# A graph network's edge loop on one core: tiles of 128 edges instead of 125, and the row-by-row and early gathers left out

## The chip, the core and the metric

The kernel runs on one core of a Trainium2 chip. The core has five engines that run side by side, each in the order of its own instructions: PE (matrix products, with weight loads shown apart as PEld), DVE (elementwise work), ACT (functions and copies), POOL (here: gathers) and SP (here: it issues DMA transfers). Sixteen DMA engines move data between HBM and the core's memory, SBUF. The metric is the device time of one execution in microseconds; less is better.

## The reference

One layer of a graph network with attention, on 12,500 nodes of 64 features and 412,500 edges, sorted by receiver:

```python
h = jnp.maximum(_layernorm(x, axis=-1), 0.0)
msg_in = jnp.concatenate([h[src], h[dst], edge_attr_32], axis=-1)
messages = swish(msg_in @ W1 + b1) @ W2 + b2
att = softmax(swish(msg_in @ Wa1 + ba1) @ Wa2 + ba2, axis=0)   # over all edges
aggregated = segment_sum(messages * att, dst, 12500)
out = x + swish(concatenate([h, aggregated]) @ Wu1 + bu1) @ Wu2 + bu2
```

All numbers are 32-bit floats.

## The kernel before, in words

**Node stage.** The node features are normalised in chunks, and two tables of 128 numbers a node are written to HBM: `ts_d`, a node's share of the first layer as a sender, and `tr_d`, its share as a receiver. The transposed features stay in SBUF as `hT`.

**Tiles and groups.** The edges are cut into tiles of `EP` = 125, one edge to a partition, and `K` = 8 tiles make a group: 3304 tiles, 413 groups (`NG`), the last one padded. The main loop in `one_pass` goes over the groups. In iteration g it runs `begin(g)`, then `load(g + 2)` (`AHEAD` = 2), then `end(g)`, and between them the steps of `sum_up` for a group some five back. An order written out by hand (`pin`) holds PE, DVE and ACT to the order of the text.

**load(g).** POOL gathers the sender rows: one indirect DMA per tile (L608), each fetching a row of `ts_d` for every edge into the group's buffer `gs`, of which the pool `gather` has seven. SP issues, every fourth group, the transposed edge features (`eo`, L619) and the receivers' numbers (`dbs`, L622), and for every group two loads of a window of `tr_d` (`wins`, L629; three buffers). DVE turns receivers into a one-hot matrix (L636), and PE multiplies it with the window (L640) into PSUM `pe`, which gives receiver and edge shares for all eight tiles.

**begin(g), end(g).** DVE adds `pe` and `gs` (L657), ACT takes the tanh (L662). `end(g)` makes messages and attention logits on DVE (L672 to L683); after it the group's `gs` is free, and POOL may fill it for a later group.

**sum_up.** DVE makes a weight matrix (L726), PE sums the messages by receiver (L732) and projects them (L743), and DVE adds them to a running table (L757, L761).

**Tiles that POOL doesn't gather.** There are three kinds.

- In the groups of `chosen` (g % 5 is 1 or 4, from 8 to 400: 157 groups) the last tile is made by ACT: it copies one column of `hT` per edge into `cols` (L514), 125 copies in five lots, which `burst` spreads over the iterations before. `numbers` loads the senders (`num`), `places` works out the column numbers on DVE (L497 to L503), DVE keeps the half that counts (L648), and PE multiplies by `stack` (L649).
- In every eighth group (51 of them) another tile is loaded row by row: `rows` has SP issue one DMA per edge (L558), 16 a group, with the row's number read into a register first (L552). `begin` adds that tile by itself (L659).
- The first `RAW` = 4 groups gather rows of `x` itself (L171), before the node stage has written `ts_d`, and `features` repeats the normalisation for those edges on DVE, ACT and PE (L579 to L593, L644).

So POOL gathers 3304 - 157 - 51 - 32 = 3064 tiles from `ts_d` and 32 from `x`. After the loop the update is made for all nodes and written out; a second function, `general`, runs only if the receivers don't fit the windows, which they do here.

Of the kernel before, what the change touches and what calls it, by code (L numbers as in the profile page):

```python
# [44 lines left out]
F32 = mybir.dt.float32  # L45
I32 = mybir.dt.int32
AF = mybir.ActivationFunctionType
# [7 lines left out]
EP = 125  # L55
# [18 lines left out]
LOTS = ((0, 24), (24, 24), (48, 24), (72, 24), (96, EP - 96))  # L74
ROUNDS = 5
SLOTS = {1: ((5, 1), (4, 0), (4, 1), (3, 0), (3, 1)), 4: ((5, 0), (5, 1), (4, 0), (4, 1), (3, 0))}
ROUND = 12582912.0
QUEUES = [(ENG.SP, 8, 0, 16)]
RAW = 4
# [12 lines left out]
def gnn_kernel(ctx: ExitStack, tc: tile.TileContext, n_edges, x, src, src_row, dst, dst_row, first, edge,  # L92
# [73 lines left out]
    raw_src = const.tile([P, RAW * K], I32, name="raw_src")  # L166
    nc.scalar.dma_start(raw_src, src[:, :RAW * K])
    raws = [gather.tile([P, K, C], F32, name="gs") for _ in range(RAW)]
    for g in range(RAW):
        for j in range(K):  # L170
            nc.gpsimd.indirect_dma_start(  # L171
                out=raws[g].rearrange("p k c -> p (k c)")[:EP, j * D:(j + 1) * D], out_offset=None, in_=x[:, :],
                in_offset=bass.IndirectOffsetOnAxis(ap=raw_src[:EP, g * K + j:g * K + j + 1], axis=0))

    with tc.tile_pool(name="node1", bufs=1) as node1, \
# [41 lines left out]
        eps = const.tile([P, 1], F32, name="eps")  # L217
# [186 lines left out]
def one_pass(tc, n_edges, v):  # L404
# [17 lines left out]
    with ExitStack() as ctx:  # L422
# [43 lines left out]
        with tc.tile_pool(name="work2", bufs=2) as work2, \  # L466
# [3 lines left out]
            pes, gss, lgs, ps_, psums, sps, pps, ees, mts, nums, cols, alone = ({} for _ in range(12))  # L470
# [11 lines left out]
            chosen = {g for g in range(8, NG - 12) if g % ROUNDS in SLOTS}  # L482

            def numbers(g):
                if g in chosen:
                    e = (g * K + K - 1) * EP
                    n = nums[g] = small.tile([P, EP], I32, name="num", bufs=3)
                    nc.sync.dma_start(n, bass.AP(tensor=v["src_row"].tensor,
                                                 offset=v["src_row"][:, e:].offset, ap=[[0, P], [1, EP]]))

            def places(g):
                if g not in chosen:
                    return
                n = nums[g]
                near = small.tile([1, EP], F32, name="near", bufs=1)
                to = small.tile([1, EP], I32, name="to", bufs=3)
                pin(nc.vector.tensor_scalar(to, n[0:1], 1, None, op0=ALU.logical_shift_right))  # L497
                m = NB // 2
                pin(nc.vector.tensor_scalar(near, to, 1.0 / m, 0.5 / m - 0.5, op0=ALU.mult, op1=ALU.add))
                pin(nc.vector.tensor_scalar(near, near, ROUND, None, op0=ALU.add))  # L500
                pin(nc.vector.tensor_scalar(near, near, ROUND, float(1 - m * P), op0=ALU.subtract, op1=ALU.mult))
                pin(nc.vector.scalar_tensor_tensor(to, to, float(P), near, op0=ALU.mult, op1=ALU.add))
                pin(nc.vector.tensor_scalar(n, n, 1, None, op0=ALU.bitwise_and))  # L503
                cols[g] = small.tile([P, EP], F32, name="cols", bufs=3), to
# [11 lines left out]
            def burst(g, k):  # L516
                for i in (3, 4, 5):
                    slots = SLOTS.get((g + i) % ROUNDS, ())
                    if (i, k) in slots:
                        columns(g + i, *LOTS[slots.index((i, k))])  # L520

            rows_at = {}
            dma = {ENG.SP: nc.sync, ENG.Activation: nc.scalar}

            def single(q, g):

                if g < NG - 4:
                    t = g * K + K - 1 - (g in chosen)
                    rows_at[q, g] = small.tile([1, EP], I32, name=f"one_src{q}", bufs=2)
                    nc.sync.dma_start(rows_at[q, g], v["src_row"][:, t * EP:(t + 1) * EP])  # L530

            def rows(q, g):
                engine, every, phase, n_rows = QUEUES[q]
                if g == 0:
                    single(q, phase + every)
                if g < phase:
                    return
                at = (g - phase) % every
                g = g - at + every
                if at == 0:  # L540
                    rows_at.pop((q, g - every), None)
                    if (q, g) in rows_at:
                        alone[g] = work2.tile([EP, C], F32, name=f"one_gs{q}")
                if at == every // 2:
                    single(q, g + every)
                if (q, g) not in rows_at:
                    return
                a = at * n_rows
                n = min(n_rows, EP - a)
                if n <= 0:  # L550
                    return
                loads, regs = nc.values_load_multi_w_load_instructions(  # L552
                    rows_at[q, g][0:1, a:a + n], engines=[engine], min_val=0, max_val=NP - 1,
                    skip_runtime_bounds_check_because=WHY)
                for one in loads:
                    pin(one)
                for k in range(n):
                    pin(dma[engine].dma_start(alone[g][a + k:a + k + 1, :], ts_d[bass.ds(regs[k], 1), :]))  # L558
# [15 lines left out]
            def features(g):  # L574

                gs = gss[g] = v["raws"][g][:EP]
                xg, xm = (gs[:, h * H:(h + 1) * H, :].rearrange("p k (r d) -> p (k r) d", d=D) for h in range(2))
                total = small.tile([EP, K], F32, name="raw_t", bufs=1)
                pin(nc.vector.tensor_reduce(total, xg, AX.X, ALU.add))  # L579
                pin(nc.vector.scalar_tensor_tensor(xm, total[:, :, None].to_broadcast([EP, K, D]), -1.0 / D, xg,  # L580
                                                   op0=ALU.mult, op1=ALU.add))
                pin(nc.scalar.activation(xg, xm, AF.Square))
                rstd = small.tile([EP, K], F32, name="raw_r", bufs=1)
                pin(nc.vector.tensor_reduce(rstd, xg, AX.X, ALU.add))
                pin(nc.scalar.activation(rstd, rstd, AF.Sqrt, bias=v["eps"][:EP], scale=1.0 / D))
                pin(nc.vector.reciprocal(rstd, rstd))
                pin(nc.vector.scalar_tensor_tensor(xg, xm, 0.0, rstd[:, :, None].to_broadcast([EP, K, D]),
                                                   op0=ALU.max, op1=ALU.mult))
                pt = one_ps.tile([P, 4, P], F32, name="mt")[:, :, :EP]
                for q in range(H):  # L590
                    pin(nc.tensor.transpose(pt[:, q, :], xg[:, 2 * q:2 * q + 2, :], ident[:EP, :EP]))
                to = raw_to[g] = v["raws"][g][:, H:, :EP]
                pin(nc.scalar.copy(to, pt))  # L593

            raw_to = {}

            def load(g):
# [4 lines left out]
                if g < RAW:  # L602
                    features(g)
                else:
                    gss[g] = gather.tile([P, K, C], F32, name="gs")[:EP]
                gs = gss[g]
                for j in range(0 if g < RAW else K - (g in chosen) - (g in alone)):
                    nc.gpsimd.indirect_dma_start(  # L608
                        out=gs[:, j, :], out_offset=None, in_=ts_d[:, :],
                        in_offset=bass.IndirectOffsetOnAxis(ap=src_sb[:, t + j:t + j + 1], axis=0))  # L610
# [20 lines left out]
                for q in range(len(QUEUES)):  # L631
                    if QUEUES[q][0] == ENG.SP:
                        rows(q, g)
# [5 lines left out]
                for q in range(H):  # L639
                    pin(nc.tensor.matmul(pe[:, 2 * q:2 * q + 2, :], eo[:, q * EP:(q + 1) * EP],  # L640
                                         win[:, q // 2, :, :], start=True,
                                         stop=g >= RAW and (q < H - 1 or g not in chosen)))
                    if g < RAW:
                        pin(nc.tensor.matmul(pe[:, 2 * q:2 * q + 2, :], raw_to[g][:, q, :], v["w_pair"][:, 0],  # L644
                                             start=False, stop=True))
# [5 lines left out]
            def begin(g):  # L651

                n = K - (g in chosen) - (g in alone)
                if g < RAW:
                    pin(nc.vector.tensor_copy(gss[g], pes[g]))
                else:
                    pin(nc.vector.tensor_tensor(gss[g][:, :n, :], pes[g][:, :n, :], gss[g][:, :n, :], ALU.add))  # L657
                if g in alone:
                    pin(nc.vector.tensor_tensor(gss[g][:, n, :], pes[g][:, n, :], alone.pop(g), ALU.add))  # L659
                if g in chosen:  # L660
                    pin(nc.vector.tensor_copy(gss[g][:, K - 1, :], pes[g][:, K - 1, :]))
# [565 lines left out]
```

## Time and profile before

| | us |
|---|---|
| median of 3 runs | 5791.38 (5784.13 to 5810.84) |
| the profiled execution | 5784.13 |
| its span, first to last instruction | 5782.4 |
| POOL's first and last gather from `ts_d` start at | 57.8 and 5679.9 |
| 16 row loads of L558, in the stretch read closely | 11.46 |
| 8 row loads of L558, a little later | 3.18 |

One line of the page is one group of instructions: its line in the code, engine, operation, what it writes and reads, the count; then the time it was busy and the mean of one in ns; then the time its engine sat idle just before, and what ended most of that. "Issue" is idle time in which the engine waited for nothing that the profile shows. The DVE's and PE's largest groups, and the DMA issues next to the row loads, are these:

```profile
L640 PE MATMUL pe<-wins,eo 128*125 128x256 f32 x3304 | 1527.2, 640 | 2546.7 <-DMA wins<-tr_d 1886.0
L726 DVE TENSOR_SCALAR wt<-iota_w,dloc,p 125x40 f32<-125x40 f32 x3304 | 759.4, 348 | 1.2
L662 ACT ACTIVATE pe<-gs 125x1024 f32<-125x1024 f32 x413 | 424.1, 1027 | 625.5 <-DMA gs<-ts_d,src_sb 189.0
...
eo<-in_edge_dram SPq DMA_DIRECT2D x103, 500.0 KB
dbs<-in_dst_row_dram SPq DMA_DIRECT2D x206, 250.0 KB
```

### The profile page before, as it was taken

To read this page: it belongs to the slowest core of one execution; us is meant where nothing else is said; L and a number is where in the kernel's file an instruction comes from. 1 tells how busy PE (TensorE), PEld (TensorE's weight loads), DVE (VectorE), ACT (ScalarE), POOL (GpSimd) and SP (SyncE) were. 2 spreads that over 40 slices of the span, in tenths; PEclk is the share of its full clock that TensorE was granted. 3 is DMA by queue.
4 is the path that set the end of the run, shared out by engine and by line. 5 is a ranking of instruction groups with operands and counts; after the bars stand their busy time and mean duration, and the time that the engine had idled before them with its cause. 6 is when DMAs were issued, how large, how long until landed. Compare 5 with 4: busy or idle time off the path is not lost. (4 is left out here: it accounts for less than half of the span.)

```text
span 5782.4 us, 108561 instructions
## 1 busy us (share of the span) xinstructions
PE 2468.3 (43%) x11609; PEld 2002.9 (35%) x11609; DVE 3466.3 (60%) x10072; ACT 2776.3 (48%) x20891; POOL 3778.6 (65%) x3121
## 2 busy tenths in 40 slices
PE   5344444444344443443444443433444443434345
PEld 4333333333333333333333333333333333333335
DVE  6565656656566655565656555655665566556657
ACT  3444444444445455454545544545455455445522
POOL 6665666666666666666667666766666666666673
PEclk8555655566555555656555556656655655655656
DMA  6233232332322223232223222222223232222233
GB/s 207 59 72 68 66 68 68 68 71 65 71 59 67 61 63 67 59 64 66 61 61 68 60 65 64 63 62 65 60 64 67 58 65 66 59 65 63 61 68 94
DMA packets 386990, 396.88 MB, mean 69 GB/s; under 512 B 235374, under 2 KB 316910, under 8 KB 385846
## 3 DMA queue, kind: packets, MB, share of 16 engines
q0 software_dynamic: 246656, 200.72, 15.9%
q1 hardware_dynamic: 138054, 179.47, 13.7%
q10 hardware_dynamic: 1520, 9.68, 0.4%
q14 instruction: 665, 5.45, 0.3%
q8 instruction: 95, 1.56, 0.1%
HBM read 360.43 MB, written 25.72 MB: 67 GB/s over the span
## 5 line engine op out<-in xcount | busy, mean ns | idle before, releaser
L608 POOL DMA_INDIRECT gs<-ts_d,src_sb x3064 | 3717.1, 1213 | 1906.6 <-issue 1794.0
L514 ACT COPY cols<-hT 128x1 f32 x19625 | 2184.3, 187 | 2078.5 <-issue 1994.7
L640 PE MATMUL pe<-wins,eo 128*125 128x256 f32 x3304 | 1527.2, 640 | 2546.7 <-DMA wins<-tr_d 1886.0
L640 PEld LDWEIGHTS pe<-wins,eo 128*125 128x125 f32 x3304 | 1017.5, 324 | 2842.9 <-issue 1835.6
L726 DVE TENSOR_SCALAR wt<-iota_w,dloc,p 125x40 f32<-125x40 f32 x3304 | 759.4, 348 | 1.2
L662 ACT ACTIVATE pe<-gs 125x1024 f32<-125x1024 f32 x413 | 424.1, 1027 | 625.5 <-DMA gs<-ts_d,src_sb 189.0
L732 PE MATMUL sp<-wt,acts 125*65 125x40 f32 x6608 | 657.7, 272 | 28.8 <-DVE wt L726 28.4
L732 PEld LDWEIGHTS sp<-wt,acts 125*65 125x65 f32 x6608 | 622.4, 188 | 35.6 <-DVE wt L726 30.0
L672 DVE SCALAR_TENSOR_TENSOR acts<-pe,gs 125x512 f32<-125x512 f32 x413 | 284.6, 689 | 408.5 <-issue 264.1
L497 DVE TENSOR_SCALAR to<-num 1x125 int32<-1x125 int32 x157 | 40.7, 259 | 778.7 <-DMA num<-in_src_row_dram 748.1
L657 DVE TENSOR_TENSOR gs<-pe,gs 125x1024 f32<-125x1024 f32 (+2 forms) x409 | 471.1, 1152 | 34.6 <-issue 10.8
L743 PEld LDWEIGHTS mt<-ss,w2u 65*128 65x128 f32 x826 | 211.8, 290 | 471.6 <-issue 375.8
L743 PE MATMUL mt<-ss,w2u 65*128 65x40 f32 x826 | 197.4, 334 | 370.0 <-DVE gm L709 145.6
L636 DVE TENSOR_SCALAR eo<-dbs,bj 64x250 f32<-64x250 int32 x826 | 294.8, 387 | 78.9 <-DMA dbs<-in_dst_row_dram 66.8
L680 DVE TENSOR_TENSOR pe<-pe,w_all 125x512 f32<-125x512 f32 x413 | 288.9, 699 | 13.8
L678 DVE SCALAR_TENSOR_TENSOR pe<-pe,gs 125x512 f32<-125x512 f32 x413 | 287.4, 696 | 10.7
L683 DVE TENSOR_REDUCE lg<-pe 125x8 f32<-125x512 f32 x413 | 284.2, 688 | 10.7
L761 DVE TENSOR_TENSOR sums<-sums,mt 64x40 f32 x606 | 115.2, 190 | 163.9 <-PE mt L743 78.6
L648 DVE SCALAR_TENSOR_TENSOR cols<-num,half,cols 128x125 f32<-128x125 int32 x157 | 54.9, 349 | 236.3 <-ACT cols L514 128.3
L764 DVE COPY stand<-nmax 64x40 f32 x826 | 186.9, 226 | 4.1 <-issue 0.8
L702 PE MATMUL mt<-ident,mx 125*128 125x125 f32 x110 | 44.6, 406 | 292.7 <-DVE sums L761 166.4
L738 ACT COPY ss<-sp 65x40 f32<-65x40 f32 x413 | 75.5, 183 | 152.3 <-remote 120.8
(140 smaller groups left out, 1230.6 us busy)
## 6 DMA issues: line engine op xcount, KB each, us to landing
one_gs<-ts_d SPq DMA_DIRECT2D x6375, 0.5 KB
eo<-in_edge_dram SPq DMA_DIRECT2D x103, 500.0 KB
dbs<-in_dst_row_dram SPq DMA_DIRECT2D x206, 250.0 KB
gs<-ts_d,src_sb POOLq DMA_INDIRECT x3064
wins<-tr_d SPq DMA_DIRECT2D x826, 32.0 KB
num<-in_src_row_dram SPq DMA_DIRECT2D x157, 62.5 KB
ts_d<-ts SPq DMA_DIRECT2D x5, 896.0 KB
tr_d<-tr ACTq DMA_DIRECT2D x5, 896.0 KB
```

What stands on the lines that cost most here:

```text
L514: pin(nc.scalar.copy(to[:, first + i:first + i + 1], hT[:, bass.ds(regs[i], 1)]))
L608: nc.gpsimd.indirect_dma_start(out=gs[:, j, :], out_offset=None, in_=ts_d[:, :], in_offset=bass.IndirectOffsetOnAxis(ap=src_sb[:, t + j:t ...
L636: pin(nc.vector.tensor_scalar(eo[:WR, e], db[:, e], bj[g // NQ % 2 * WR:(g // NQ % 2 + 1) * WR, g, h:h + 1], None, op0=ALU.is_equal))
L640: pin(nc.tensor.matmul(pe[:, 2 * q:2 * q + 2, :], eo[:, q * EP:(q + 1) * EP], win[:, q // 2, :, :], start=True, stop=g >= RAW and (q < H - ...
L657: pin(nc.vector.tensor_tensor(gss[g][:, :n, :], pes[g][:, :n, :], gss[g][:, :n, :], ALU.add))
L662: pin(nc.scalar.activation(pes[g], gss[g], AF.Tanh))
L672: pin(nc.vector.scalar_tensor_tensor(acts[g % ACTS][:, :, 0:U], th[:, :, U:C], 1.0, gs[:, :, U:C], op0=ALU.add, op1=ALU.mult))
L678: pin(nc.vector.scalar_tensor_tensor(att, th[:, :, 0:U], 1.0, gs[:, :, 0:U], op0=ALU.add, op1=ALU.mult))
L680: pin(nc.vector.tensor_tensor(att, att, wa2[:EP, None, :].to_broadcast([EP, K, U]), ALU.mult))
L726: pin(nc.vector.tensor_scalar(wt[:, j, :], iota_w[:EP, j // H, :], dloc[:, g * K + j:g * K + j + 1], p[:, k + j:k + j + 1], op0=ALU.is_equ ...
L732: pin(nc.tensor.matmul(sp, acts[g % ACTS][:, j, :], wt[:, j, :], start=j == 0, stop=j == K - 1))
L743: pin(nc.tensor.matmul(pp, w2u.rearrange("s h u -> s (h u)"), sps.pop(g), start=True, stop=True))
```

## The change

Four things change.

- `EP` becomes 128. There are 403 groups and 3224 tiles; every gather has 128 rows.
- The groups whose last tile ACT makes are one in three (`EVERY` = 3, `PHASE` = 1, groups 10 to 388: 127 of them). Six lots of 12 to 24 columns are spread over three iterations, two an iteration. `num`, `to` and `cols` have two buffers instead of three.
- The row-by-row tiles are taken out (`single`, `rows`, `QUEUES`, `alone`).
- The early gathers from `x` are taken out (`RAW`, `raws`, `features`, the extra products in `load`).

POOL gathers 3224 - 127 = 3097 tiles, all from `ts_d`. The words for the change also name the update's bias from node features in SBUF and `x` rows asked for ahead; those parts stand in both kernels alike.

```diff
-EP = 125
+EP = 128
...
-LOTS = ((0, 24), (24, 24), (48, 24), (72, 24), (96, EP - 96))
-ROUNDS = 5
-SLOTS = {1: ((5, 1), (4, 0), (4, 1), (3, 0), (3, 1)), 4: ((5, 0), (5, 1), (4, 0), (4, 1), (3, 0))}
+EVERY = 3
+PHASE = 1
+SLOTS = (((0, 24), (24, 24)), ((48, 24), (72, 12)), ((84, 24), (108, 20)))
...
-QUEUES = [(ENG.SP, 8, 0, 16)]
-RAW = 4
...
-    raw_src = const.tile([P, RAW * K], I32, name="raw_src")
-    nc.scalar.dma_start(raw_src, src[:, :RAW * K])
-    raws = [gather.tile([P, K, C], F32, name="gs") for _ in range(RAW)]
-    for g in range(RAW):
-        for j in range(K):
-            nc.gpsimd.indirect_dma_start(
...
-            chosen = {g for g in range(8, NG - 12) if g % ROUNDS in SLOTS}
+            chosen = {g for g in range(8, NG - 12) if g % EVERY == PHASE}
...
             def burst(g, k):
-                for i in (3, 4, 5):
-                    slots = SLOTS.get((g + i) % ROUNDS, ())
-                    if (i, k) in slots:
-                        columns(g + i, *LOTS[slots.index((i, k))])
-
-            rows_at = {}
...
-                for k in range(n):
-                    pin(dma[engine].dma_start(alone[g][a + k:a + k + 1, :], ts_d[bass.ds(regs[k], 1), :]))
+                for i in range(EVERY):
+                    columns(g + 3 + i, *SLOTS[EVERY - 1 - i][k])
...
-            def features(g):
...
-                if g < RAW:
-                    features(g)
-                else:
-                    gss[g] = gather.tile([P, K, C], F32, name="gs")[:EP]
-                gs = gss[g]
-                for j in range(0 if g < RAW else K - (g in chosen) - (g in alone)):
+                gs = gss[g] = gather.tile([P, K, C], F32, name="gs")[:EP]
+                for j in range(K - (g in chosen)):
...
-                for q in range(len(QUEUES)):
-                    if QUEUES[q][0] == ENG.SP:
-                        rows(q, g)
...
-                    if g < RAW:
-                        pin(nc.tensor.matmul(pe[:, 2 * q:2 * q + 2, :], raw_to[g][:, q, :], v["w_pair"][:, 0],
-                                             start=False, stop=True))
...
-                n = K - (g in chosen) - (g in alone)
-                if g < RAW:
-                    pin(nc.vector.tensor_copy(gss[g], pes[g]))
-                else:
-                    pin(nc.vector.tensor_tensor(gss[g][:, :n, :], pes[g][:, :n, :], gss[g][:, :n, :], ALU.add))
-                if g in alone:
-                    pin(nc.vector.tensor_tensor(gss[g][:, n, :], pes[g][:, n, :], alone.pop(g), ALU.add))
...
+                n = K - (g in chosen)
+                pin(nc.vector.tensor_tensor(gss[g][:, :n, :], pes[g][:, :n, :], gss[g][:, :n, :], ALU.add))
```

## The prediction

> **What bounds the kernel now.** I read the page's span and group rows first, then the waits of all engines, then SP's own waits, then the timeline of a stretch in mid-loop, and last the durations of the gather's line.
>
> ```profile
> span 5782.4 us, 108561 instructions
> PE 2468.3 (43%) x11609; PEld 2002.9 (35%) x11609; DVE 3466.3 (60%) x10072; ACT 2776.3 (48%) x20891; POOL 3778.6 (65%) x3121
> L608 POOL DMA_INDIRECT gs<-ts_d,src_sb x3064 | 3717.1, 1213 | 1906.6 <-issue 1794.0
> L514 ACT COPY cols<-hT 128x1 f32 x19625 | 2184.3, 187 | 2078.5 <-issue 1994.7
> ...
> one_gs<-ts_d SPq DMA_DIRECT2D x6375, 0.5 KB
> ```
> POOL does little but gather (L608). Each gather is 1.213 us and is followed by at least 0.305 us in which POOL waits for nothing the profile names, so one costs 1.518 us and 3064 cost 4651 us. They run from 57.8 to 5681.1 us, which is 5623 us: POOL has 972 us to spare, all of it ahead of the first gather of a group, where it waits for one of seven `gs` buffers. So POOL is close to the bound and isn't it. ACT's column copies (L514) take 2184 us busy and 1995 us of "issue" between them (their register loads): 4179 us, or 0.213 us a column. With its other work ACT has 2776 + 2085 = 4861 us.
>
> ```profile
> PE pe L640 <- DMA wins<-tr_d: 1886.0, 274, 16.2
> POOL gs L608 <- issue: 1794.0, 2933, 16.6
> ...
> SPq L558 <- DMA one_gs<-ts_d: 63.8, 152, 0.8
> SPq L558 <- DMA dbs<-in_dst_row_dram: 37.6, 46, 1.7
> ```
> The longest wait on another party is PE's: 1886 us for `wins`, a load that SP issues. SP's own waits, by contrast, come to some 290 us in the whole span (the two longest in its loop are shown). An engine whose products are waited for and that hardly waits itself sets the pace.
>
> ```profile
> 3002.65 1.46 SPq L629 DMA_DIRECT2D wins<-tr_d  x2
> 3005.20 11.46 SPq L558 DMA_DIRECT2D one_gs<-ts_d  x16
> 3010.02 1.21 POOL L608 DMA_INDIRECT gs<-ts_d,src_sb  x1 [1.56 <-issue]
> 3018.13 0.77 SPq L629 DMA_DIRECT2D wins<-tr_d  x2
> 3019.89 3.18 SPq L558 DMA_DIRECT2D one_gs<-ts_d  x8
> 3020.06 3.75 PE L640 MATMUL pe<-wins,eo 128*125 128x256 f32 x8 [7.21 <-DMA wins<-tr_d]
> ```
> This shows why. Sixteen single-row loads (L558) stand in SP's order between two groups' window loads. They took 11.46 us here (0.72 us each) and elsewhere 0.40 us each (eight in 3.18), out of a group's mean 5623/409 = 13.75 us. PE gets its window 7.21 us late, `begin`, `end` and the freeing of `gs` follow, and POOL pays at its next group.
>
> **The change, part by part.**
>
> *SP's rows go.* 6375 row loads, their 51 index loads and 408 register loads leave SP's order; at 0.40 to 0.72 us a row that is 2550 to 4590 us. What stays is two window loads a group, the edge and receiver loads every fourth group, and the numbers: under 4 us a group by the stretch above. The window is no longer late, and the 972 us of POOL's waits lose their main cause. What comes late next is whichever of POOL and ACT has more to do. The 51 tiles go back to POOL.
>
> *Columns in one group of three.* 127 groups instead of 157, 128 columns instead of 125: 16,256 copies instead of 19,625. ACT saves 3369 x 0.213 = 717 us and keeps 4144 us, 10.3 us a group. This hides behind POOL as long as POOL needs more than that. 30 tiles go back to POOL. `num` and `cols` have two buffers instead of three; a chosen group's are last read in `load`, two groups ahead of it, and the next but one asks for them only then, so I cost this at nothing; if the cover failed, SP would hold the next window back, as now.
>
> *Tiles of 128.* 403 groups instead of 413, 3224 tiles instead of 3304. PE, DVE and ACT do about the same per group (three more rows of partitions, matmuls of 128 columns instead of 125), so each saves 10/413 of its group work: 84 us of DVE's 3466. None of it is on the path.
>
> *The early gathers from x go.* 32 gathers that POOL made from 3.8 to 56.3 us, while `ts_d` was still being written (its last write is issued at 50.7 us), become 32 gathers after it. DVE, ACT and PE lose the four groups' `features`, off the path. The first gather from `ts_d` no longer stands behind them: I take 54 us for it (50.7 us and about 3 to land) instead of 57.8.
>
> *The sum of gathers.* 3224 - 127 = 3097 of 128 rows, against 3064 of 125 and the 32. POOL's work after `ts_d` is thus 3097 gathers at a price which decides everything.
>
> *The price of a 128-row gather.* No row shows one. These are the nearest:
>
> ```profile
> L608 POOL DMA_INDIRECT gs<-ts_d,src_sb x3064: 1205/1212/1549, 57.8 to 5679.9; - x192
> L171 POOL DMA_INDIRECT gs<-in_x_dram,raw_src x32: 1208/1212/3515, 3.8 to 56.3; - x32
> q0 software_dynamic: 246656, 200.72, 15.9%
> ```
> L171 gathers rows of 256 bytes and L608 of 512, at the same median of 1212 ns: bytes cost POOL nothing. Rows grow by 2.4% only. The packets say what does change. Of that queue's 246,656, each `ts_d` gather left 15 of 4096 bytes (eight rows) and 5 of 512 bytes (one row): five equal shares of 25 rows on five DMA engines. The other eleven got filler, 25 descriptors of 4 bytes each. 125 can be shared equally over 5 or 25; 128 over 2, 4, 8 or 16. If POOL's time goes by the engines that get rows, the price is at most 1212 x 16/5 = 3878 ns. If it writes all 16 engines in step, a descriptor each, the steps fall from 26 (with the closing one) to 9 and it is 1212 x 9/26 = 420 ns. Going by rows alone it is 1212 x 128/125 = 1241 ns. Bytes and rows being excluded as a large effect, the engines served are what changes by a factor, and I take it that more of them cost more. For the size I take the longest gather that L608 itself shows, 1549 ns, some 31 ns for each of eleven more engines; nothing from the far end, 242 ns an engine, supports more.
>
> The Trainium skill ("DMA: Bandwidth & Descriptors", section "Why a DMA increments its semaphore by 16 and not by 1") says that a transfer is spread over the largest number of engines, up to 16, that divides its outer size: 5 for 125 and 16 for 128. The packets agree for 125; no run here shows 128. The same page (section "Anatomy of one DMA") calls descriptor generation a small cost, with many descriptors before it shows; by that a gather stays at 1212 ns, the sum would be about 4.9 ms, and the rule speaks against my forecast.
>
> *The end.* 54 us + 3097 x (1.549 + 0.305) = 5742 us + the tail, from the last gather to the end, as now: 5782.4 - 5681.1 = 101 us. POOL then needs 14.2 us a group against ACT's 10.3, so few waits remain. I keep those now put down to ACT's columns and DVE's L680 (51.7 + 20.7 us), cut to 127/157: 60 us. That makes 5957 us of span against 5782.4. The profiled execution took 5784.13 us around its span; the median of the runs, 5791.38, lies 9 us above the span, so I forecast 5965 us.
>
> **The rivals.**
>
> *1. The gather's price goes by rows (the other side).* At 1241 ns a gather costs 1.546 us, all of them 4788 us, with head and tail 4943. POOL's 11.9 us a group stand close to ACT's 10.3, so I add 150 us of waits: about 5100 us. The constancy of 1212 ns over half the bytes speaks for it; the 16 engines speak against. It decides below a price of (5782.4 - 54 - 101 - 60)/3097 - 0.305 = 1.493 us; above that the kernel is slower.
>
> *2. The price falls.* With 420 ns POOL needs 2245 us and ACT is the bound. Its columns run from 148 us to 225 us ahead of the end now; 3462 us of them and some 560 of ACT's other 682 us (4861 - 4179), the rest lying at both ends, give 4400 us without a wait, and with waits of one us a group about 4800. The filler descriptors speak for it, the lack of any cheaper gather in the trace against.
>
> *3. SP's rows were hidden anyway.* If ACT or the chain through DVE kept the 13.75 us a group, 403 groups take 5541 us, with head and tail 5700. SP's short waits speak against.
>
> **How the numbers follow.** The forecast has 0.70: more work on POOL per gather. Rival 1 has 0.16, rival 2 0.08, rival 3 0.03, and 0.03 is left for a price within some 10 ns of 1.493 us. Two runs of this kernel differ by up to 0.5%, so no change means within 29 us. Faster is the three rivals, 0.27; same 0.03; slower 0.70. The forecast's own range is 5800 us (just past the deciding price) to 6450 (45 ns an engine, half as much again: 1.707 us a gather, 54 + 3097 x 2.012 + 101 + 60 = 6446). The whole range reaches down to 5050, which takes in rival 1 and leaves out rival 2 and the far tail above, some 2 in 10.
>
> **What would show it.** Right: the gather's row near 1.5 us or more, POOL's idle time near 3097 x 0.305 = 945 us, PE's wait for `wins` a small part of 1886 us, SP idle, 16,256 column copies. Wrong: a gather of 1.25 us or less, with POOL's waits for buffers small (rival 1) or ACT without idle time (rival 2); or windows still late with SP free (rival 3). A gap after each gather other than 0.305 us would move the sum by 31 us for every 10 ns.

## The result and the profile after

The changed kernel took 6004.51 us (median; 6000.57 to 6005.61), the kernel before beside it 5787.76 us (5773.24 to 5810.84). The ratio is 1.037, 95% interval [1.033, 1.040]: slower, by some 217 us. That is the record of the first runs, on one chip. On two chips met later the same two kernels have a ratio of 0.833; the experiments tell how far that can be explained.

The page of the changed kernel, its span, engine row, the rows of the gathers and of ACT's column copies, and the gathers' DMA queue:

```profile
span 6003.9 us, 80416 instructions
...
PE 2571.5 (43%) x11238; PEld 1997.6 (33%) x11238; DVE 3276.5 (55%) x9553; ACT 2408.1 (40%) x17477; POOL 2957.4 (49%) x3122
...
q0 software_dynamic: 99104, 203.16, 13.6%
...
L530 POOL DMA_INDIRECT gs<-ts_d,src_sb x3097 | 2940.2, 949 | 2956.7 <-issue 2880.1
L503 ACT COPY cols<-hT 128x1 f32 x16256 | 1851.3, 188 | 3085.7 <-issue 3046.2
```

A 128-row gather takes POOL 949 ns, not more than the 1213 of 125 rows but less. Its 3097 gathers, each with the 0.305 us behind it, are work for 3884 us; POOL is idle for 2957 us all the same, 2012 us more than those gaps. No engine is busy for more than 55% of the span. The packets confirm how a gather is spread: 99,104 over 3097 gathers are 32 each, 16 of 4096 bytes (eight rows) and 16 of 4 bytes, so each of the 16 engines gets eight rows. A gather of 125 rows left 80.

The waits of all engines in the same kernel (total, times, longest, in us):

```profile
ACT cols L503 <- issue: 3046.2, 3441, 2.9
POOL gs L530 <- issue: 2880.1, 3006, 31.6
...
PE mt L654 <- ACT ss L649: 1384.0, 156, 19.9
...
PE pe L559 <- DMA wins<-tr_d: 57.8, 1, 57.8
```

The 1886 us in which PE waited for windows are gone; what is left of them is one wait at the start. In their place PE waits for ACT, ACT for "issue", and POOL up to 31.6 us for a buffer. A column copy now costs (1851.3 + 3085.7)/16,256 = 0.304 us, against 0.217 before (2184.3 + 2078.5 over 19,625), with the copy itself unchanged at 188 ns. The timeline of a stretch shows where ACT's time lies:

```profile
3010.48 0.19 ACT L503 COPY cols<-hT 128x1 f32 x1 [1.22 <-issue]
3010.80 0.95 POOL L530 DMA_INDIRECT gs<-ts_d,src_sb  x1 [0.30 <-issue]
3011.88 0.19 ACT L503 COPY cols<-hT 128x1 f32 x1 [1.21 <-issue]
3012.06 0.95 POOL L530 DMA_INDIRECT gs<-ts_d,src_sb  x1 [0.30 <-issue]
...
3023.83 0.65 PE L654 MATMUL mt<-ss,w2u 65*128 65x40 f32 x2 [11.54 <-ACT ss L649]
...
3024.36 2.13 ACT L503 COPY cols<-hT 128x1 f32 x22 [0.58 <-issue]
...
3025.86 0.94 POOL L530 DMA_INDIRECT gs<-ts_d,src_sb  x1 [9.11 <-issue]
```

While POOL gathers, one every 1.25 us, ACT gets one copy done in 1.4 us. When POOL has run out of buffers, 22 copies take 2.13 us (the full pace is back at 3019.6 us, 2.9 us after the run's last gather ended). The instructions are the same. ACT is held between them, and what it owes to PE (`ss`, L649) and DVE comes late, so POOL's buffers come free late.

### The profile page after: what moved, and what is told of

Same layout as the page of the kernel before. It is cut to its first block, busy times and chain, and to the rows that moved or that the text cites. A ratio compares the mean times of both kernels' runs of the same rounds, so it can differ in the third digit from the quotient of the medians.

```text
span 6003.9 us, 80416 instructions
## 1 busy us (share of the span) xinstructions
PE 2571.5 (43%) x11238; PEld 1997.6 (33%) x11238; DVE 3276.5 (55%) x9553; ACT 2408.1 (40%) x17477; POOL 2957.4 (49%) x3122
## 3 DMA queue, kind: packets, MB, share of 16 engines
q0 software_dynamic: 99104, 203.16, 13.6%
## 5 line engine op out<-in xcount | busy, mean ns | idle before, releaser
L530 POOL DMA_INDIRECT gs<-ts_d,src_sb x3097 | 2940.2, 949 | 2956.7 <-issue 2880.1
L503 ACT COPY cols<-hT 128x1 f32 x16256 | 1851.3, 188 | 3085.7 <-issue 3046.2
L559 PE MATMUL pe<-wins,eo 128*128 128x256 f32 x3224 | 1493.4, 639 | 860.1 <-DVE eo L555 413.2
L559 PEld LDWEIGHTS pe<-wins,eo 128*128 128x128 f32 x3224 | 985.5, 323 | 1172.8 <-DVE eo L555 450.3
L637 DVE TENSOR_SCALAR wt<-iota_w,dloc,p 128x40 f32<-128x40 f32 x3224 | 723.6, 311 | 21.9 <-issue 20.1
L643 PE MATMUL sp<-wt,acts 128*65 128x40 f32 x6448 | 722.9, 293 | 15.5 <-issue 12.5
L643 PEld LDWEIGHTS sp<-wt,acts 128*65 128x65 f32 x6448 | 689.9, 213 | 16.8 <-issue 13.2
L570 DVE TENSOR_TENSOR gs<-pe,gs 128x1024 f32<-128x1024 f32 (+1 forms) x403 | 474.6, 1178 | 66.3 <-issue 52.3
L573 ACT ACTIVATE pe<-gs 128x1024 f32<-128x1024 f32 x403 | 412.1, 1023 | 230.3 <-issue 80.5
L591 DVE TENSOR_TENSOR pe<-pe,w_all 128x512 f32<-128x512 f32 x403 | 281.8, 699 | 16.2 <-issue 2.2
```

What stands on the lines that cost most here:

```text
L503: pin(nc.scalar.copy(to[:, first + i:first + i + 1], hT[:, bass.ds(regs[i], 1)]))
L530: nc.gpsimd.indirect_dma_start(out=gs[:, j, :], out_offset=None, in_=ts_d[:, :], in_offset=bass.IndirectOffsetOnAxis(ap=src_sb[:, t + j:t ...
L573: pin(nc.scalar.activation(pes[g], gss[g], AF.Tanh))
L591: pin(nc.vector.tensor_tensor(att, att, wa2[:EP, None, :].to_broadcast([EP, K, U]), ALU.mult))
L637: pin(nc.vector.tensor_scalar(wt[:, j, :], iota_w[:EP, j // H, :], dloc[:, g * K + j:g * K + j + 1], p[:, k + j:k + j + 1], op0=ALU.is_equ ...
L643: pin(nc.tensor.matmul(sp, acts[g % ACTS][:, j, :], wt[:, j, :], start=j == 0, stop=j == K - 1))
```

## The experiments

After the result the question was whether the 128-row gathers themselves hold the other engines back, or whether ACT's columns, in one group of three, had become the bound by themselves. e1 and e4 change the size of a tile alone, e2 takes the columns away and e3 SP's rows. Each group of runs sent together shared a chip, with the kernel before beside it, and the four groups went to four different chips; the record doesn't say which chip the first runs had. The kernel before took 5807 us there for e1 to e4 (much as on the first), 5368 for e5 to e8, 4787 for e9 to e11 and 4788 for e12.

**e1: the change, with 125 edges a tile.**

```diff
-EP = 128
+EP = 125
-SLOTS = (((0, 24), (24, 24)), ((48, 24), (72, 12)), ((84, 24), (108, 20)))
+SLOTS = (((0, 24), (24, 24)), ((48, 24), (72, 12)), ((84, 24), (108, 17)))
```

> The changed kernel with tiles of 125 edges alone put back (413 groups, 3173 gathers, 131 groups with columns). Theory A (ACT's column copies are the bound of the changed kernel, and the 128-row gather on more DMA engines makes a copy dearer, 0.301 us instead of 0.213): the copy falls back to about 0.21 us, ACT needs some 3500 us for 16,375 of them, and the time falls to 5000 to 5300 us. Theory B (the copy became dearer because SP's rows are gone, whatever the gather): it stays near 0.30 us and the time stays within 2% of 6004 us. Gather 1.213 us in both.

Measured 4975.13 us, ratio to before 0.857 [0.855, 0.859]: 25 us under theory A's range, and far from theory B's. The page of this kernel:

```profile
L530 POOL DMA_INDIRECT gs<-ts_d,src_sb x3173 | 3842.5, 1211 | 1058.5 <-issue 1010.9
L503 ACT COPY cols<-hT 128x1 f32 x16375 | 1878.4, 188 | 1884.2 <-issue 1823.3
```

A column costs (1878.4 + 1884.2)/16,375 = 0.230 us. POOL's idle time is hardly more than its gaps (3173 x 0.305 = 968 us): with the median gather of 1.209 us, 3173 x 1.514 and some 155 us at the ends are 4959 us. On this chip everything in the change but the size of the tile was worth 14%; set against the first chip's 6004.51 us, the size cost all of it and more.

**e2: the changed kernel without ACT's columns** (`chosen = set()`; POOL gathers all 3224 tiles).

> The changed kernel with no groups chosen: ACT makes no columns, POOL gathers all 3224 tiles. If ACT's columns are the bound, POOL takes over: 3224 x (0.949 + 0.305) = 4043 us, with head and tail about 4200 to 4400 us. If POOL, or the chain through PE and DVE, set the pace of the changed kernel (POOL has 1965 us of waits there, so this rival needs the chain), 127 more gathers bring no gain: 5900 us or more.

Measured 5610.79 us, 0.967 [0.965, 0.969]. Neither expectation was met. ACT has 591.5 us of work in it, POOL 3224 x (0.945 + 0.305) + 155 = 4185 us, and yet 1426 us more pass. The timeline of a stretch of this kernel:

```profile
3005.70 1.73 PE L643 MATMUL sp<-wt,acts 128*65 128x40 f32 x16
...
3008.40 1.03 ACT L573 ACTIVATE pe<-gs 128x1024 f32<-128x1024 f32 x1 [6.48 <-DVE gs L570]
...
3013.88 0.95 POOL L530 DMA_INDIRECT gs<-ts_d,src_sb  x1 [0.30 <-issue]
...
3027.63 0.94 POOL L530 DMA_INDIRECT gs<-ts_d,src_sb  x1 [0.30 <-issue]
3033.19 0.19 ACT L649 COPY ss<-sp 65x40 f32<-65x40 f32 x1 [23.77 <-remote]
3033.43 0.65 PE L654 MATMUL mt<-ss,w2u 65*128 65x40 f32 x2 [21.29 <-ACT ss L649]
```

PE's `sp` is done at 3007.43 us, ACT is free at 3009.43, and ACT's copy of `sp` starts at 3033.19, 4.6 us after POOL's last gather of the run ended. PE's last work between them ends at 3012.14 us, DVE's at 3017.25; from there on only POOL works. The view puts 23.77 us of the wait down to "remote", which names no party. But the copy waits for the count that PE's matmuls raise, and SP's next window load, which waits for the same count, starts at 3032.94 us, beside the copy. The rises of that count which the trace holds for this stretch lie at 3008.88, 3013.18, 3028.56 and from 3032.07 to 3032.92 us. So the hold isn't in ACT's register loads alone: here the signal of matmuls long done came late, for two engines at once.

**e3: the kernel before, without SP's rows** (`QUEUES = []`), and **e4: the kernel before, with 128 edges a tile** (`EP = 128`).

> The kernel before without SP's row-by-row tiles (POOL gathers those 51 tiles too, 3115 from the sender table). If SP's order alone set the pace: PE's wait for windows vanishes, POOL needs 3115 x 1.518 = 4729 us, the time falls to 4950 to 5300 us. If ACT's columns come next and grow dearer once SP is out of the way (0.30 us x 19,625 = 5890 us), the time does not fall: 5800 to 6600 us.

> The kernel before with tiles of 128 edges alone (rows, two columns groups in five and early gathers kept). If a 128-row gather is cheaper by itself the gather shows 0.95 us. If SP's rows set the pace, 50 tiles of 128 rows cost what they did: 5700 to 5850 us. If the gather on more engines makes ACT's copies dearer (0.30 us for some 19,500), the time grows past 6100 us.

e3: 5012.32 us, 0.864 [0.862, 0.866]. e4: 6947.43 us, 1.197 [1.194, 1.199]. Page of e3, then page and longest waits of e4:

```profile
L608 POOL DMA_INDIRECT gs<-ts_d,src_sb x3115 | 3779.7, 1213 | 1101.3 <-issue 1027.0
```

```profile
L608 POOL DMA_INDIRECT gs<-ts_d,src_sb x2990 | 2834.2, 948 | 3966.4 <-issue 3723.2
```

```profile
PE pe L640 <- DMA wins<-tr_d: 2821.2, 248, 28.6
ACT cols L514 <- issue: 2777.9, 3214, 3.0
```

e3 met its first expectation. e4 is past the 6100 us of a gather that holds ACT up, though a copy there costs (2142.6 + 2843.9)/19,584 = 0.255 us and not 0.30. Without rows POOL's waits nearly vanish; with 128-row gathers the windows come later still, 2821 us of waiting in place of 1886. The two parts stand apart: rows away is -14%, 128 rows a gather is +20% (both on this chip), and +21% where the rows are gone (the first chip's 6004.51 against e1's 4975.13).

**e5: a pause between the gathers.**

```diff
                         in_offset=bass.IndirectOffsetOnAxis(ap=src_sb[:, t + j:t + j + 1], axis=0))
+                    nc.gpsimd.memset(pause, 0.0)
```

> The changed kernel with one GpSimd memset of 128x128 f32 after each gather (0.2 us in the rows so far), so that gathers of 128 rows follow each other every 1.5 us instead of every 1.25 us, near the 1.518 us of the 125-row gathers. Theory A (128-row gathers one behind the other leave the other engines no room for their semaphore updates and next instructions; it is the back-to-back pace that holds them up): POOL works 3097 x 1.5 + 155 = 4800 us, the holds go, and the time falls from 6004 to 4900-5200 us although POOL has more to do. Theory B (each 128-row gather costs the others the same, whatever the pace): 6000 us or more, ACT's columns stay near 0.30 us each. Halfway between (5300-5800): pace is part of it only.

Measured 6469.29 us, 1.205 [1.200, 1.210], and the time answers nothing: all 3097 memsets ran between 122.9 and 1478.5 us, where only 414 gathers fell, so they paused no later gather. The 2634 gathers behind them took 4990 us to the end, 1.89 us each, which is the pace of the changed kernel on the first chip ((5898.3 - 49.7)/3096 = 1.889).

Its trace does answer something. In the stretch with the memsets most gathers came in bursts of seven or eight, 1.25 us apart, with some 50 memsets behind each burst. Here are ACT's copies from 123 to 1478 us, and from 1500 to 5700 us of the same execution (views by line of ACT in these two windows):

```profile
L504 ACT COPY cols<-hT 128x1 f32 x2352 | 233.2, 187 | 111.2 <-issue 108.2 <-DVE pe L591 2.9
```

```profile
L504 ACT COPY cols<-hT 128x1 f32 x12362 | 1408.0, 188 | 2277.3 <-issue 2249.8 <-DMA gs<-ts_d,src_sb 8.9 <-PE sp L645 5.3
```

A column costs 0.146 us in the first stretch and 0.298 us in the second, with the same gathers of 128 rows. With breaks between short bursts the hold is all but gone; most copies of the first stretch lie in the breaks, though (all but 131), so how the hold builds up within a run has to be counted. The table has the share of ACT's register operations (one stands ahead of each copy, 37 ns by the median) that took over 100 ns, by the time since POOL's run of gathers began; gathers less than 0.5 us apart are one run. The columns for 126, 121 and 119 edges are from e6, e7 and e8 below:

| us since the run began | 128, first chip | 126 | 121 | 119 | 125, e1 |
|---|---|---|---|---|---|
| 0 to 2.5 | 3% | 1% | 2% | 0% | 0% |
| 2.5 to 5 | 11% | 4% | 6% | 4% | 0% |
| 5 to 7.5 | 40% | 26% | 22% | 14% | 3% |
| 7.5 to 10 | 68% | 51% | 35% | 10% | 11% |
| 10 to 15 | 92% | 65% | 53% | 25% | 9% |
| 15 to 20 | 99% | 74% | 51% | 29% | 13% |

For 128 rows the hold sets in after some 5 us of unbroken gathers and grows to nearly every operation; for 125 rows it stays at about one in eight. So a gather doesn't cost the others a fixed amount, whatever came before it.

**e6, e7, e8: tiles of 126, 121 and 119 edges** (the changed kernel, `EP` and the last slot alone).

> The changed kernel with tiles of 126 edges: 410 groups, some 3150 gathers, 126 = 14 engines x 9 rows. From 1212 ns at 25 rows an engine and 949 ns at 8, some 15.5 ns for each row of an engine: this gather should take about 965 ns, and one every 1.27 us. Theory A (the hold comes from gathers of few steps over many engines, back to back): 5700-6100 us, ACT's columns near 0.30 us. Theory B (only gathers over all 16 engines hold the others, since then no engine is left free): POOL needs 3150 x 1.27 + 155 = 4155 us, ACT some 4200 us of its own, and the time is 4400-4800 us.

> The changed kernel with tiles of 121 edges: 427 groups, some 3280 gathers, 121 = 11 engines x 11 rows. By 15.5 ns a row of an engine the gather takes about 1.0 us, one every 1.30 us, POOL 3280 x 1.30 + 155 = 4420 us. Theory A (many engines, back to back, hold the others; by degrees): between the 4975 us of 125 and the 6004 us of 128, 5300-5800 us. Theory B (only all 16 engines hold): 4500-4900 us, POOL and ACT (16,335 columns at 0.213 us and 700 us else, 4180 us) both close to the bound. Were the gather's time not by steps, its row shows it: 1.2 us again.

> The changed kernel with tiles of 119 edges: 434 groups, some 3334 gathers, 119 = 7 engines x 17 rows. By 15.5 ns a row of an engine the gather takes about 1.09 us, one every 1.40 us, POOL 3334 x 1.40 + 155 = 4820 us. Theory A (by degrees of the engines served): a little of the hold, 4900-5200 us. Theory B (only all 16 engines hold): POOL-bound, 4820-4950 us, and faster than the 4975 us of 125 although it has 161 more gathers.

Measured 5918.12, 5919.59 and 5721.61 us, ratios to before on their chip 1.103 [1.098, 1.108], 1.103 [1.098, 1.108] and 1.066 [1.061, 1.071]. The durations of the gathers (minimum, median, maximum), in the order 126, 121, 119:

```profile
L530 POOL DMA_INDIRECT gs<-ts_d,src_sb x3150: 991/997/1282, 50.8 to 5808.2; - x197
```

```profile
L530 POOL DMA_INDIRECT gs<-ts_d,src_sb x3281: 1018/1023/1406, 49.8 to 5792.1; - x193
```

```profile
L530 POOL DMA_INDIRECT gs<-ts_d,src_sb x3334: 1098/1102/1507, 51.1 to 5615.7; - x197
```

The packets show the shares. A gather of 126 rows left 14 of 4096 bytes and 14 of 512, one of 121 rows 11 of 4096 and 11 of 1536, one of 119 rows 14 of 4096 and 7 of 512: 9 rows on each of 14 engines, 11 on 11, 17 on 7. They lie between 8 rows (128, 946 ns) and 25 (125, 1209 in e1). From 9 rows to 25 the price rises by 13.3 ns a row ((1209 - 997)/16; the two between lie within 2 ns of that line), and 8 rows lie 38 ns below it. So the price of a gather follows the rows an engine gets, and most of it, by that line some 878 ns, is fixed. The time beyond POOL's own work, n x (median + 0.305) + 155, is 876 us for 119 (7 engines, a gather every 1.41 us), 1407 for 121 (11 engines, 1.33 us) and 1662 for 126 (14 engines, 1.30 us). Theory B of these runs (all 16 engines alone hold the others) falls. Theory A's range holds for 126 alone; 121 and 119 came out above theirs (5300 to 5800 and 4900 to 5200 us). Whether the number of engines or the pace does it, these runs can't tell, since both rise together.

**e9: the pause, in order; e10: the best of the 125-row parts; e11: the changed kernel on their chip.**

```diff
-                    nc.gpsimd.indirect_dma_start(
+                    pin(nc.gpsimd.indirect_dma_start(
...
+                    pin(nc.gpsimd.memset(pause, 0.0))
```

e10 is the kernel before with `QUEUES = []` and the change's columns:

```diff
...
-QUEUES = [(ENG.SP, 8, 0, 16)]
+QUEUES = []
...
-            chosen = {g for g in range(8, NG - 12) if g % ROUNDS in SLOTS}
+            chosen = {g for g in range(8, NG - 12) if g % EVERY == PHASE}
...
```

> The changed kernel with the memset again, this time with gathers and memsets held in program order on GpSimd (in the run before, the planner drew all memsets into the first 1480 us, so that it paused nothing). One gather of 128 rows every 1.25 + 0.205 + some 0.05 = 1.5 us. Theory A (the pace of the gathers sets the hold): inside POOL's runs ACT spends 0.25-0.35 of the time in steps over 0.5 us, as with 125 rows (0.24; every 1.514 us), against 0.63 in the changed kernel; total 4850-5200 us. Theory B (each gather costs the others by the engines that it is spread over, whatever the pace): the slow steps stay at some 1.0 us a gather (125 rows: 0.36, 119: 0.65, 121: 0.86, 126: 0.99, 128: 1.02), and the time is 5700-6200 us.

> The kernel before without SP's rows and with columns in one group of three: 125-row gathers, and 32 early gathers from x kept. POOL has 3141 gathers after the table is written: 58 + 3141 x 1.516 + 101 = 4920 us with hardly a wait. Both theories: 4900-4960 us on the chip of the first runs, faster than all before. Were the hold of the other engines' steps to grow with the copies or with the early gathers, it would come out at 4975 us (125 rows in the changed kernel) or more.

> The changed kernel itself, on the chip of the other two: 6000 us if the chip plays no part. The kernel before took 5368 us on the chip that ran the sizes 119, 121 and 126, and 5790-5807 us on the others; should the changed kernel also differ by hundreds of us between chips, the sizes are compared by their own rows only.

Measured 4319.50, 4898.69 and 3989.39 us; before beside them 4787.10 us, so 0.902 [0.901, 0.904], 1.023 [1.022, 1.025] and 0.833 [0.832, 0.835]. For e11, 6000 us was expected if the chip plays no part; that was off by a third: on this chip the change is a gain of 17%. The page of e11:

```profile
span 3988.2 us, 80416 instructions
...
q0 software_dynamic: 99104, 203.16, 20.5%
...
L530 POOL DMA_INDIRECT gs<-ts_d,src_sb x3097 | 2936.1, 948 | 993.1 <-issue 865.7
...
L503 ACT COPY cols<-hT 128x1 f32 x16256 | 1605.0, 187 | 718.1 <-issue 715.2
```

The gather takes 948 ns as on the first chip, the copy 187, and the queue's packets 20.5% of 3988.2 us, which is 818 us against 13.6% of 6003.9, 817 us. Neither these instructions nor the transfers are faster here. The clock granted to PE is higher, 0.645 against 0.570, but PE's busy time differs by 245 us (2326.2 against 2571.5), a small part of the 2016 us between the spans. What went are the steps between: ACT's 3086 us of idle time ahead of copies became 718, and POOL's idle time is its gaps (3097 x 0.305 = 945 us) and the 48 us ahead of the first gather. Counted over the whole trace, ACT took over 0.5 us from one instruction's start to the next's, without a wait of its own, some 4300 times on the first chip (some 3160 us in all, 77% of the steps inside POOL's runs of gathers) and 723 times here (705 us). The clearest rows are those of the register operation that stands ahead of each copy, minimum/median/maximum in ns; first the changed kernel on the first chip, then e11:

```profile
L503 ACTq FUSED_REGOPS  x16256: 3/37/1449, 173.1 to 5753.6; - x199
```

```profile
L503 ACTq FUSED_REGOPS  x16256: 37/37/43, 124.0 to 3773.0; - x199
```

An operation that takes 37 to 43 ns here took up to 1449 on the first chip. The kernel before had it too, there on SP, in the rows' line:

```profile
L558 SPq MOVE one_gs<-ts_d x6375: 2/29/732, 91.7 to 5664.5; - x200
```

The pause (e9) met a chip without the hold, so neither of its theories was tested. It costs 330 us (4319.5 - 3989.4), or 0.107 us a gather: about half of the memset's mean 226 ns must have gone into the gap that was there anyway. e10 is 112 us slower than the kernel before, and that is its 77 further gathers (3141 against 3064, x 1.517 = 117 us). So on this chip SP's rows had been hidden work, and taking them away is a loss.

**e12: the changed kernel once more.**

> The changed kernel once more, on the chip of this call, whichever that is. Theory C (on some chips, or at some times, the other engines' steps of 0.7 us come in masses while gathers run, on others they don't; the kernel before and the changed one feel the same hold, the changed one more): where the kernel before takes 5790-5810 us, near 6000 us, a ratio of 1.03-1.04, and ACT's columns near 0.30 us each; where it takes 4790 us, near 3990 us, 0.83, and 0.143 us a column; where it takes some 5370 us, 5500-5900 us, 1.03-1.10. Theory D (a chip shifts the changed kernel only by chance of the moment, the kernel before on its own grounds): the two don't go together, for instance 5800 us before and 4000 us after.

Measured 3987.25 us, before 4788.00 us, 0.833 [0.832, 0.834], on a further chip. A column costs (1605.0 + 719.3)/16,256 = 0.143 us. Theory C's numbers for such a chip are met within 0.1%; what it says of the other sorts wasn't met with again.

The runs without a pause in one table, with POOL's own work worked out as n x (median + 0.305) + 155 us:

| before there | kernel | POOL's work | time | beyond it |
|---|---|---|---|---|
| 5788 | changed, 128 | 4029 | 6005 | 1975 |
| 5807 | e1, 125 | 4959 | 4975 | 16 |
| 5807 | e2, 128, no columns | 4185 | 5611 | 1426 |
| 5807 | e3, 125, no rows | 4874 | 5012 | 138 |
| 5807 | e4, 128, with rows | 3892 | 6947 | 3055 |
| 5368 | e8, 119 | 4846 | 5722 | 876 |
| 5368 | e7, 121 | 4512 | 5920 | 1407 |
| 5368 | e6, 126 | 4256 | 5918 | 1662 |
| 4787 | e10, 125 | 4911 | 4899 | -12 |
| 4787 | e11, changed | 4023 | 3989 | -34 |
| 4788 | e12, changed | 4023 | 3987 | -36 |

By the same sum the kernel before needs 58 + 3064 x 1.518 + 101 = 4810 us: it took 4787 and 4788 on the last chips, and 5788 on the first. With 125 rows the hold is there too, on a chip that has it: ACT sat idle 1884 us ahead of its copies in e1 and 747 in e10. POOL's longer work covers it.

## Why the prediction came out as it did

The forecast, 5965 us, lies 40 us from the 6004.51 of the first chip, and its direction holds there. Its reason doesn't: two errors of the sum, 1858 us too much and 1906 too little, cancel. That the number was met is luck.

*The price of a 128-row gather* is the step that failed: "For the size I take the longest gather that L608 itself shows, 1549 ns". It is 949 ns, so that term was 3097 x 0.600 = 1858 us too high. More engines don't cost POOL more; fewer rows on each cost it less. By the prediction's own deciding price, 1.493 us, such a gather makes the kernel faster, as it did on the last chips. Rival 2 had the direction, from the filler descriptors, but put the whole 1212 ns on the steps and came to 420. The page "DMA: Bandwidth & Descriptors" of the Trainium skill ("Anatomy of one DMA") calls descriptor generation a small cost that shows only with many descriptors. The medians (1102, 1023, 997 and 946 ns at 17, 11, 9 and 8 rows an engine, 1209 at 25) agree in that most is fixed, and differ in that a few rows already show.

*Waits of 60 us* were left in the sum; on the first chip they were 6003.9 - 49.7 - 3097 x 1.254 - 105 = 1966 us. The forecast holds no term for what took the price's place: the other engines are held between instructions while such gathers run. That it is the gathers' shape and not something else of the change is shown on that sort of chip by e1 and e4, which change the size alone.

*SP's rows set the pace before*: right on the first chip. PE's wait for windows fell from 1886 to 57.8 us and e3 gains 14%. But 0.40 to 0.72 us a row was taken as a row's own price, and the upper part of it was the hold again (a MOVE of 29 ns taking up to 732). Where the hold is absent, the kernel before runs at POOL's work and the rows are hidden, which is rival 3's premise; e10 shows it by its 112 us.

*ACT keeps 10.3 us a group, behind POOL*: wrong on the first chip, since a column there went from 0.217 to 0.304 us and ACT's products came late. On the last chips it costs 0.143 us, and with 125-row gathers (e10) (1617.4 + 747.1)/16,375 = 0.144. So of the 0.217 us before (0.213 in the prediction, for copies and their register loads), a third was the hold.

*The gap of 0.305 us, the head and the tail* held: gathers follow each other at 0.30, the first starts at 49.7 us (54 taken), the last ends 105 us ahead of the end (101 taken).

*The signals* named for the forecast split accordingly. PE's small wait for `wins` and the 16,256 copies came; the gather at 1.5 us and POOL idle near 945 us did not. POOL's idle time near 945 us did come on the last chips, beside a gather of 0.95 us: the sum with the right price is 54 + 3097 x 1.254 + 101 + 60 = 4099 us, against 3988.

What stays open: what holds the engines. The traces show it as steps of about 0.7 us and more on ACT and SP, mostly inside POOL's runs of gathers; they show no copy and no gather that is slower, and no more time in the gathers' packets. They show no cause for a chip to have it or not, and whether a chip keeps it was not tried; as the first chip isn't known, it may even be one of those met later. That it builds up over an unbroken run of gathers is shown; the number of engines served and the pace of the gathers weren't told apart. One rival was not tested at all: that the recording of the profile holds the engines. Every timed execution was recorded, and the traces from chips with the hold miss records: for 7218 DVE instructions that raise a count, the first chip's trace has 4340 records of a rise, e11's 7090. What the kernels take without a recording isn't known.

## What to carry to other kernels

Read minimum, median and maximum of the cheapest instructions (register operations, moves) before taking a stretch's pace as an engine's price: here an operation of 37 ns reached 1449 where ACT was held and 43 where it wasn't, and a cost per row or column read in a held stretch is not a property of the code. Between 25 and 8 rows on a DMA engine a gather was cheaper the fewer rows each engine got, so a row count that shares over 16 engines is worth trying, but where the hold is present it can cost more than it brings. A gain or loss that rests on such holds should be measured on more than one chip before it is believed: here the same change was 3.7% slower in the first runs and 16.7% faster on two chips later.

## What the runs showed of the hardware

- The same program took 6005 us in the first runs and 3989 and 3987 us on two chips later, with equal durations of gathers (949 and 948 ns), copies (188 and 187 ns) and gather packets (817 and 818 us in all). On the two latter chips the seven runs each of the kernel before lie within 0.1%.
- A gather of 128 rows leaves 32 packets, one of 125 rows 80, and takes POOL 946 ns against 1209.
- Where the hold was present, the time beyond POOL's work in the changed kernel goes up with the engines that a gather is shared over, from 16 us (125 rows) over 876 (119), 1407 (121) and 1662 (126) to 1975 us (128). 119, 121 and 126 ran on one chip, where the kernel before took 5368 us, the other two sizes where it took 5807 and 5788. Where the hold wasn't, there is none for 125 or 128 rows.
- The hold builds up: in the changed kernel's first runs 3% of ACT's register operations were lengthened in the first 2.5 us of a run of gathers, 99% from 15 to 20 us.
- In e2 a copy that waited for a finished matmul started 24 us after ACT was free, and for the last 16 us of that only POOL had worked, 11 of them with gathers.
